# Dealing each expert's features six to a partition in a fused state-space and mixture-of-experts layer on Trainium2

## The chip, the cores and the metric

The kernel runs on one NeuronCore of one Trainium2 chip. The metric is the device time of one execution in microseconds (us). A core has five engines with instruction streams of their own: TensorE (PE in the profile, with its weight loads listed apart as PEld), VectorE (DVE), ScalarE (ACT), GpSimd (POOL) and SyncE (SP, which here only issues transfers). All numbers are float32.

## What is computed

There are 16 sequences of 256 tokens with 256 channels. For each the output is the input plus two branches, both fed by the layer-normed input `xn`:

```
xn = layernorm(x)
x  = x + ssm(xn) + moe(xn)

# ssm: proj, causal conv (4 taps), silu, then a scan over time with 512 features x 16 states
dts = softplus(dt @ W_dt + b_dt);  dA = exp(dts * A);  dBu = dts * Bm * hs
state = dA * state + dBu ;  y = sum_n state * C
out_ssm = ((y + hidden * D) * silu(gate)) @ W_out

# moe: 32 experts of 96 features, the 8 best of a softmax router per token
for e in range(32):
    w_e = sum(where(sel == e, rw, 0))
    acc += (silu(xn @ w_gate[e]) * (xn @ w_up[e])) @ w_down[e] * w_e
```

The change is in the second branch. The 32 x 96 = 3072 expert features of all experts are computed for every token; the routing weight `w_e` of a token (zero for an expert that it didn't choose) scales the features of expert e.

## The kernel before

One sequence is one round `b` of 16. Features lie on the 128 partitions, tokens along the free dimension. The 3072 expert features are 24 chunks of 128, and PE, ACT, POOL and DVE work on pairs of chunks `q` (12 pairs a round). Four groups `g` of 8 experts (768 features, 6 chunks, `CPG` = 6) share one tile of routing weights.

A pair goes through these steps. `gates` (line 496, two pairs at once) and `ups` (`expand`, line 483) multiply the transposed input `xnT` by the gate and up weights: four matmuls a pair and kind, with a 128x128 slice of the resident weights `wg_sb` or `wu_sb` as the loaded (stationary) operand and 256 tokens moving (line 490). `silu` (line 500) takes the gate product from PSUM to `sg` on ACT; `weigh` (line 506) multiplies `sg` by the routing weights `wr` on POOL; `combine` (line 511) multiplies by the up product into `h` on DVE; `down` (line 517) multiplies `h` by `wd_sb` and adds into `acc` over the whole round (line 525).

The routing weights of a round are computed with tokens on partitions, transposed on DVE, and written to a small array in device memory by four transfers (`send_weights`, line 456). `spread` (line 467) then reads them back so that each partition holds the row of the expert whose feature it carries. A chunk has 128 features and an expert 96, so chunks and experts don't meet: chunk 0 holds expert 0 and a third of expert 1, and so on. The pattern repeats after 4 experts and 3 chunks, so a group takes six transfers, of 32, 64 or 96 partitions, each of which fills two chunks. The tile is 128 x 6 x 256 numbers, with a ring of two tiles.

The state-space branch runs beside this: `project`, `conv_first`, `conv_rest`, `activate`, `params`, `widen` and `steps` prepare a round; `fetch` (line 634) spreads two states' rows of B and C over all partitions by a 512 KB transfer (`rep`, a ring of three tiles); `feed` (line 646) multiplies on POOL; `decay` (line 655) is the exponential on ACT; `scan` and `read` (lines 668 and 676) run on DVE; `collect` (line 686) adds to `y` by an accumulating transfer that POOL issues; `gate`, `fold`, `gated` and `project_out` finish it. `load_again`, `settle`, `finish` and `store` add the input and write the result.

The order of instructions on every engine comes from a planner that runs while the program is built. The class `Plan` (line 20) takes the steps with an engine, an assumed length, a due time, what they need, and which ring buffers they take and give back; it plays them forward and, whenever an engine is free, starts the ready step with the earliest due time (line 86). The due time is a base time (`ORIGIN`, `PERIOD`, `RATE`, `LEAD`) plus a constant for the kind of step, from the tables `DUE`, `FIRST` (first round), `SECOND` and `LAST`; `EARLY` says how long before its due time a step may become ready. The result is a fixed order for each engine; on the chip the instructions wait for each other by semaphores.

SP issues all loads and stores and the transfers of `spread`, `fetch`, `send_weights` and `send_params`, in the planned order. At the start it issues the first input (`load_x`), then router and projection weights, and later the expert weights in four groups of three kinds (`load_experts`, line 298).

Of the kernel before, what the change touches and what calls it, by code (L numbers as in the profile page):

```python
# [120 lines left out]
def mamba_moe_kernel(  # L121
# [30 lines left out]
    nc = tc.nc  # L152
    P = 128
    B, L, H = x.shape
# [4 lines left out]
    NE, _, I = w_gate.shape  # L159
# [6 lines left out]
    AHEAD = 3  # L166
# [3 lines left out]
    PARTS = 4  # L170
    EPG = NE // PARTS
    CPG = FC // PARTS
# [3 lines left out]
    SPP = SLOTS // PARTS  # L176
    FAR = 1e30
    SLOWEST = 1e-26
    ORIGIN = -7.2
    PERIOD = 79.1  # L180
    RATE = 79.0

    DUE = dict(
        load_x=-300.5, stats=-15.5, root=132.5, invert=-162.0, center=-75.0, norm=244.0,
        turn=-535.0, keep_turned=-94.0, route=-100.0, largest=-231.5, expo=221.0, choose=-1192.5,
        send_weights=-260.5, project=-51.5, conv_first=455.5, conv_rest=185.0, activate=-293.5,
        params=-209.0, keep_params=-266.0, send_params=-303.5, widen=-273.0, steps=-79.0,
        skip=120.0, inputs=-299.5, fetch=-252.5, feed=315.5, decay=-34.0, scan=539.0, read=55.9,
        collect=-257.0, spread=65.5, gates=-25.5, ups=669.0, silu=245.5, weigh=233.0,
        combine=-138.5, down=288.0, settle=-496.5, gate=50.5, gate_silu=216.0, fold=502.5,  # L190
        gated=894.5, project_out=-81.0, load_again=-68.0, finish=160.0,
    )
    EARLY = dict(
        load_x=175.0, load_experts=25.0, stats=37.0, turn=1.0, route=277.0, project=671.0,
    )

    FIRST = dict(
        route=179.5, largest=36.5, expo=-163.5, choose=655.5, project=409.0, conv_first=-563.0,
        conv_rest=-561.0, activate=218.5, params=-266.5, keep_params=285.0, widen=-51.5,
        steps=971.5, skip=-377.0, inputs=295.0, fetch=-161.5, feed=-360.0, decay=-135.0, scan=36.5,  # L200
        read=33.0, collect=-157.0, spread=-263.5, gates=-97.5, ups=-247.0, silu=-204.0,
        weigh=270.0, combine=402.0, down=53.0,
    )

    SECOND = dict(
        load_x=-132.5, stats=-1.0, root=-131.0, invert=-137.5, center=-86.0, norm=251.0,
        turn=267.0, keep_turned=-305.5, route=89.0, largest=-27.5, expo=-14.0, choose=46.0,
        send_weights=8.0, project=267.5, conv_first=36.5, conv_rest=-36.5, activate=-61.0,
        params=26.0, keep_params=178.5, send_params=13.0, widen=126.5, steps=-25.0, skip=225.5,
        inputs=-138.5, fetch=-56.0, feed=24.0, decay=7.0, scan=104.0, read=31.5, collect=-154.0,  # L210
        spread=8.0, gates=1.5, ups=-251.0, silu=46.5, weigh=-137.5, combine=48.0, down=100.5,
        settle=-112.0, gate=-10.0, gate_silu=-83.0, fold=99.0, gated=-152.0, project_out=-44.0,
        load_again=-35.0, finish=22.5,
    )

    LAST = dict(
        fetch=-123.0, feed=-25.0, decay=359.0, scan=571.0, read=-65.0, collect=-281.5,
        spread=-131.0, gates=216.5, ups=75.5, silu=445.0, weigh=-274.5, combine=448.0, down=296.5,
        settle=-10.0, gate=-75.5, gate_silu=105.5, fold=-115.5, gated=339.0, project_out=-460.5,
        finish=479.0,  # L220
    )
    LEAD = -28.0
    TOPK = 8
    EPS = 1e-5

# [5 lines left out]
    sb = ctx.enter_context(tc.tile_pool(name="sb", bufs=1))  # L231
# [2 lines left out]

    RINGS = dict(
        sk=1, xt=1, mv=1, st=1, std=1, xnT=3, nmax=1, rest=1, dt=1, hs=2, dts=2, y0=2, y1=2,
        rep=3, bu=3, pr=4, da=AHEAD, g=2, u=2, acc=1, wr=2, sg=3, h=2, gs=2, o=1,
    )
    taken = defaultdict(int)

    def take(pool, ring, shape, nm):
        i = taken[ring] % RINGS[ring]
        taken[ring] += 1
        return pool.tile(shape, F32, tag=f"{ring}_{i}", name=nm)
# [3 lines left out]
    live = {}  # L248
# [216 lines left out]


    def spread(b, g):
        wd = live["wd", b]
        wr = take(sb, "wr", [P, CPG, L], f"wr_{b}_{g}")
        half = EPG // 2  # L470
        for e in range(half):
            lo, hi = e * I, (e + 1) * I
            while lo < hi:
                c, r = divmod(lo, P)
                n = min(hi - lo, P - r)
                nc.sync.dma_start(
                    wr[r : r + n, c :: CPG // 2, :],
                    wd[g * EPG + e : (g + 1) * EPG : half, :].partition_broadcast(n),
                )
                lo += n  # L480
        live["wr", b, g] = wr

    def expand(b, q, kind):
        xs = live["xnT", b]
        w = {"g": wg_v, "u": wu_v}[kind]
        p = bank(f"p{kind}_{b}_{q}", kind).rearrange("p (j l) -> p j l", j=2)
        for j in range(2):
            c = 2 * q + j
            for hc in range(HC):
                nc.tensor.matmul(  # L490
                    p[:, j, :], w[:, hc, ts(c, P)], xs[:, hc, :],
                    start=(hc == 0), stop=(hc == HC - 1),
                )
        live[kind, b, q] = p
# [271 lines left out]
    b = 0  # L766
# [40 lines left out]
    for b in range(B):  # L807
# [54 lines left out]
        for g in range(GROUPS):  # L862
            at = t + PERIOD / GROUPS * g
            add("fetch", (b, g), "SP", 512 * KB, at, b, g, needs=[("send_params", b)],
                takes=[("rep", ("rep", b, g))], lands=5.5, early=14.0)

        for r in range(UNITS):
            k = UNITS * b + r
# [54 lines left out]
        add("load_again", (b,), "SP", 256 * KB, t, b, takes=[("o", ("o", b))], lands=8.0, early=25.0)  # L923
# [3 lines left out]
        add("gate", (b,), "PE", 8 * MM, t, b, gives=[xT],  # L927
            takes=[(r, (r, "gate", b, q)) for q in range(2) for r in ("g", "gs")],
            needs=[("keep_turned", b)] + ([] if b else [("load_in", 1)]), early=10.0)
# [10 lines left out]
        for q in range(PAIRED):  # L940
# [5 lines left out]
            gives=[("po", b)])  # L946
        add("store", (b,), "SP", 256 * KB, t + 100.0, b, needs=[("finish", b), ("settle", b)],
            gives=[("o", b)],
            lands=7.0)
    plan.issue()  # L950


# [30 lines left out]
```

## Time and profile before

| | |
|---|---|
| time, median of 3 runs | 1308.02 us (1305.14 to 1309.28) |
| span of the profiled execution, first to last instruction | 1309.5 us |
| instructions | 18902 |
| bytes moved by transfers | 268.80 MB, 205 GB/s on average |
| queue 0 (issued by POOL) | 124.80 MB, 50.4% of the time of 16 transfer engines |
| queue 1 (issued by SP and ACT) | 142.75 MB, 40.4% |
| mean granted TensorE clock | 0.993 |

The profile is of one execution of its own, whose span stands above; the times of the three runs are whole executions without its detail. In its rows, "xcount | busy, mean ns of one" tells how many instructions of a kind there were, how long their engine was busy with them altogether, and the mean length of one. Matmuls overlap in their records, so their pace is read from the starts of successive rows rather than from the mean length. One matmul of the program is two MATMUL records, each with a weight load (LDWEIGHTS) of its own.

### The profile page before, as it was taken

To read this page: it belongs to the slowest core of one execution; us is meant where nothing else is said; L and a number is where in the kernel's file an instruction comes from. 1 tells how busy PE (TensorE), PEld (TensorE's weight loads), DVE (VectorE), ACT (ScalarE), POOL (GpSimd) and SP (SyncE) were. 2 spreads that over 40 slices of the span, in tenths; PEclk is the share of its full clock that TensorE was granted. 3 is DMA by queue.
4 is the path that set the end of the run, shared out by engine and by line. 5 is a ranking of instruction groups with operands and counts; after the bars stand their busy time and mean duration, and the time that the engine had idled before them with its cause. 6 is when DMAs were issued, how large, how long until landed. Compare 5 with 4: busy or idle time off the path is not lost.

```text
span 1309.5 us, 18902 instructions
## 1 busy us (share of the span) xinstructions
PE 1288.9 (98%) x5978; PEld 1109.9 (85%) x5978; DVE 1157.5 (88%) x1719; ACT 1133.9 (87%) x1898; POOL 1181.6 (90%) x835
## 2 busy tenths in 40 slices
PE   9979999999999999999999999999999999999998
PEld 7868888887888888888888888888888888888887
DVE  3778989999899998989899898898989899899986
ACT  5878898997989989899898989989899898998883
POOL 1778999999999989999999898999999989998995
PEclk8999999999999999999999999999999999999999
DMA  9998899899999989999998988989899989998994
GB/s 248 241 230 191 189 237 195 215 206 211 201 222 198 226 199 200 199 212 206 199 215 188 213 191 206 225 189 209 185 216 216 197 193 203 217 210 193 202 221 94
DMA packets 169940, 268.80 MB, mean 205 GB/s; under 512 B 37840, under 2 KB 103920, under 8 KB 169840
## 3 DMA queue, kind: packets, MB, share of 16 engines
q0 software_dynamic: 36576, 124.80, 50.4%
q1 hardware_dynamic: 130624, 142.75, 40.4%
q8 instruction: 47, 0.77, 0.2%
q10 hardware_dynamic: 2640, 0.05, 0.1%
q14 instruction: 53, 0.43, 0.1%
HBM read 137.51 MB, written 5.24 MB: 109 GB/s over the span
## 4 chain that ended last, share of the span: by engine, by line
PE 63%; POOL 12%; DVE 8%; issue 6%; DMA 5%; ACT 4%; SPq 1%; POOLq 0%; DVEq 0%; ACTq 0%
PE acc L525 16%; PE pg L490 16%; PE pu L490 16%; POOL bu L649 6%; POOL sg L509 4%; PE px L574 3%; PE po L742 3%; PE ph L536 3%; DVE da L671 3%; PE pgate L716 3%; DMA y<-pr 2%; POOL y L688 2%; DVE hs L559 2%; DVE pr L683 2%; ACT da L663 2%
## 5 line engine op out<-in xcount | busy, mean ns | idle before, releaser
L649 POOL TENSOR_TENSOR bu<-rep,hs 128x1024 f32<-128x1024 f32 x256 | 716.4, 2924 | 59.7 <-DMA rep<-bcd 34.2
L671 DVE TENSOR_TENSOR_SCAN da<-da,bu 128x512 f32<-128x512 f32 x512 | 609.0, 1217 | 53.0 <-ACT da L663 44.8
L663 ACT ACTIVATE da<-dts,a_sb 128x256 f32<-128x256 f32 x1024 | 469.6, 473 | 84.6 <-DVE pr L683 61.9
L490 PE MATMUL pu<-xnT,wu_sb 128*128 128x256 f32 x1536 | 362.5, 382 | 5.8 <-DVE h L513 5.5
L525 PE MATMUL acc<-wd_sb,h 128*128 128x256 f32 x1536 | 364.2, 380 | 3.9 <-DVE h L513 3.8
L490 PE MATMUL pg<-xnT,wg_sb 128*128 128x256 f32 x1536 | 348.8, 380 | 3.1 <-DVE hs L559 1.5
L490 PEld LDWEIGHTS pu<-xnT,wu_sb 128*128 128x128 f32 x1536 | 292.6, 191 | 48.0 <-DVE h L513 7.5
L490 PEld LDWEIGHTS pg<-xnT,wg_sb 128*128 128x128 f32 x1536 | 291.0, 190 | 46.1 <-ACT sg L503 2.9
L525 PEld LDWEIGHTS acc<-wd_sb,h 128*128 128x128 f32 x1536 | 291.6, 190 | 45.1 <-DVE h L513 5.1
L509 POOL TENSOR_TENSOR sg<-sg,wr 128x512 f32<-128x512 f32 x192 | 326.3, 1922 | 2.3 <-ACT sg L503 2.3
L688 POOL DMA_DIRECT2D y<-pr x222 | 299.9, 1352 | 16.6 <-DVE da L671 5.8
L683 DVE TENSOR_TENSOR pr<-da,rep 128x512 f32<-128x512 f32 x448 | 294.0, 676 | 2.7 <-DVE pr L683 0.7
L663 ACT ACT_TABLE_LOAD x151 | 193.7, 1283 | 2.6
L513 DVE TENSOR_TENSOR h<-pu,sg 128x512 f32<-128x512 f32 x192 | 131.1, 683 | 58.9 <-POOL sg L509 31.8
L503 ACT ACTIVATE sg<-pg 128x512 f32<-128x512 f32 x192 | 105.3, 594 | 4.3 <-PE pg L490 2.1
L503 ACT ACT_TABLE_LOAD x81 | 103.9, 1283 | 2.9 <-PE pg L490 1.5
L732 POOL TENSOR_TENSOR y<-y,gs 128x512 f32<-128x512 f32 x30 | 79.4, 2816 | 0.2
L559 DVE SCALAR_TENSOR_TENSOR hs<-ph,small,hs 128x255 f32<-128x255 f32 (+2 forms) x192 | 76.0, 471 | 1.9 <-ACT hs L548 1.9
L707 POOL TENSOR_TENSOR y<-y 128x512 f32<-128x512 f32 x32 | 64.6, 2347 | 0.5 <-DMA y<-pr 0.5
L536 PE MATMUL ph<-xnT,win_sb 128*128 128x256 f32 x256 | 63.4, 392 | 0.0
L742 PE MATMUL po<-wout_sb,y 128*128 128x256 f32 x256 | 60.8, 380 | 1.0 <-DVE hs L559 1.0
L574 PE MATMUL px<-hs,wx_sb 128*32 128x256 f32 (+1 forms) x256 | 61.4, 387 | 0.0
(66 smaller groups left out, 863.4 us busy)
## 6 DMA issues: line engine op xcount, KB each, us to landing
y<-pr POOLq DMA_DIRECT2D x222, 512.0 KB, 7.0
rep<-bcd SPq DMA_DIRECT2D x128, 512.0 KB, 6.6
wr<-wd SPq DMA_DIRECT2D x128, 192.0 KB, 6.6
wr<-wd SPq DMA_DIRECT2D x128, 128.0 KB, 7.1
wr<-wd SPq DMA_DIRECT2D x128, 64.0 KB, 6.7
y<-sk POOLq DMA_DIRECT2D x32, 256.0 KB, 8.1
xt<-L_attn_input_states_dram SPq DMA_DIRECT2D x16, 256.0 KB, 4.9
o<-L_attn_input_states_dram SPq DMA_DIRECT2D x16, 256.0 KB, 6.9
```

Of the source, the lines that this page charges most:

```text
L490: nc.tensor.matmul(p[:, j, :], w[:, hc, ts(c, P)], xs[:, hc, :], start=(hc == 0), stop=(hc == HC - 1),)
L503: nc.scalar.activation(sg, live.pop(("g", b, q)), AF.Silu)
L509: nc.gpsimd.tensor_mul(sg, sg, wr[:, r : r + 2, :])
L513: nc.vector.tensor_mul(h, live.pop(("u", b, q)), live.pop(("sg", b, q)))
L525: nc.tensor.matmul(acc[:, s, :], h[:, j, ts(s, P)], wd_sb[:, c, :], start=(c == 0 and s == 0), stop=(c == FC - 1), skip_group_check=True,)
L536: nc.tensor.matmul(ph[:, j, :], win_sb[:, hc, ts(2 * q + j, P)], xs[:, hc, :], start=(hc == 0), stop=(hc == HC - 1),)
L559: nc.vector.scalar_tensor_tensor(cv[:, c, k:], ph[:, j, : L - k], cw[:, c, KC - 1 - k : KC - k], cv[:, c, k:], op0=ALU.mult, op1=ALU.add,)
L649: nc.gpsimd.tensor_mul(bu, live["rep", b, g][:, 0:1].to_broadcast([P, CPU, NG, L]), live["hs", b][:, ts(u, CPU), :].unsqueeze(2).to_broadc ...
L663: nc.scalar.activation(da[:, i, :], dts[:, c, :], AF.Exp, scale=a_sb[:, c, n : n + 1])
L671: nc.vector.tensor_tensor_scan(flat, flat, live["bu", k][:, j].rearrange("p n l -> p (n l)"), 0.0, op0=ALU.mult, op1=ALU.add,)
L683: nc.vector.tensor_mul(live["pr", k][:, :, j, :], live.pop(("da", m)), live["rep", b, g][:, 1])
L688: nc.gpsimd.dma_start(live["y", b, u].rearrange("p n c l -> p (n c l)"), live.pop(("pr", k)).rearrange("p n c l -> p (n c l)"), accum_op=A ...
```

## The change

There are three parts.

1. The 768 features of a group of 8 experts are dealt to the 128 partitions six at a time: partition p holds features 6p to 6p+5 of the group, and chunk r of the group is the r-th of the six. As 6 x 16 = 96, sixteen partitions hold exactly one expert, whatever the chunk. So `wr` shrinks to one row of 256 numbers per partition, one tile serves all six chunks, and `weigh` reads it for both chunks of a pair. `wd_sb` is loaded in the same dealing, six consecutive rows to a partition. The gate and up weights stay in memory as they were; the slice of a chunk now takes every sixth column.
2. `spread` is one transfer per group, from 8 rows, each repeated 16 times. The ring of `wr` has four tiles instead of two.
3. The tables of due times, the base times, the planner's assumed lengths of a few steps and the "early" limits are all new, so the order of instructions is another. The tables now name every kind of step.

```diff
@@ base times, rings
-    ORIGIN = -7.2
-    PERIOD = 79.1
-    RATE = 79.0
+    ORIGIN = -7.07
+    PERIOD = 79.07
+    RATE = 79.73
...
-    LEAD = -28.0
+    LEAD = -11.12
...
-        rep=3, bu=3, pr=4, da=AHEAD, g=2, u=2, acc=1, wr=2, sg=3, h=2, gs=2, o=1,
+        rep=3, bu=3, pr=4, da=AHEAD, g=2, u=2, acc=1, wr=4, sg=3, h=2, gs=2, o=1,
@@ weights
-    wd_v = w_down.rearrange("e i h -> (e i) h").rearrange("(c p) h -> p c h", p=P)
+    wd_v = w_down.rearrange("e i h -> (e i) h").rearrange("(g p c) h -> p g c h", p=P, c=CPG)
...
-            nc.sync.dma_start(wd_sb[:, ts(j, CPG), :], wd_v[:, ts(j, CPG), :])
+            nc.sync.dma_start(wd_sb[:, ts(j, CPG), :], wd_v[:, j])
...
-    wg_v = wg_sb.rearrange("p c e i -> p c (e i)")
-    wu_v = wu_sb.rearrange("p c e i -> p c (e i)")
+    wg_v = wg_sb.rearrange("p c (g e) i -> p c g (e i)", g=PARTS)
+    wu_v = wu_sb.rearrange("p c (g e) i -> p c g (e i)", g=PARTS)
@@ def spread(b, g):
-        wd = live["wd", b]
-        wr = take(sb, "wr", [P, CPG, L], f"wr_{b}_{g}")
-        half = EPG // 2
-        for e in range(half):
-            lo, hi = e * I, (e + 1) * I
-            while lo < hi:
-                c, r = divmod(lo, P)
-                n = min(hi - lo, P - r)
-                nc.sync.dma_start(
-                    wr[r : r + n, c :: CPG // 2, :],
-                    wd[g * EPG + e : (g + 1) * EPG : half, :].partition_broadcast(n),
-                )
-                lo += n
+        wr = take(sb, "wr", [P, L], f"wr_{b}_{g}")
+        rows = live["wd", b][ts(g, EPG), :]
+        nc.sync.dma_start(
+            wr,
+            rows.unsqueeze(1).to_broadcast([EPG, P // EPG, L]),
+        )
@@ def expand(b, q, kind):
-            c = 2 * q + j
+            g, r = divmod(2 * q + j, CPG)
             for hc in range(HC):
                 nc.tensor.matmul(
-                    p[:, j, :], w[:, hc, ts(c, P)], xs[:, hc, :],
+                    p[:, j, :], w[:, hc, g, r::CPG], xs[:, hc, :],
@@ def weigh(b, q):
-        g, r = divmod(2 * q, CPG)
-        sg, wr = live["sg", b, q], live["wr", b, g]
-        nc.gpsimd.tensor_mul(sg, sg, wr[:, r : r + 2, :])
+        sg, wr = live["sg", b, q], live["wr", b, 2 * q // CPG]
+        nc.gpsimd.tensor_mul(sg, sg, wr.unsqueeze(1).to_broadcast([P, 2, L]))
@@ assumed lengths (and the tables DUE, EARLY, FIRST, SECOND, LAST, all numbers new)
-        add("center", (b,), "POOL", 0.15, t, b, needs=[("invert", b)], gives=[("mv", b)])
+        add("center", (b,), "POOL", 0.74, t, b, needs=[("invert", b)], gives=[("mv", b)])
...
-        add("turn", (b,), "PE", 1.0, t, b, needs=[("norm", b)], gives=[x],
+        add("turn", (b,), "PE", 0.46, t, b, needs=[("norm", b)], gives=[x],
...
-        add("choose", (b,), "DVE", 1.35, t, b, needs=[("expo", b)], gives=[("pl", b)])
+        add("choose", (b,), "DVE", 1.8, t, b, needs=[("expo", b)], gives=[("pl", b)])
...
-            add("spread", (b, i), "SP", 3.0, e + RATE / PARTS * i, b, i,
-                needs=[("send_weights", b)], takes=[("wr", ("wr", b, i))], lands=6.0, early=20.0)
+            add("spread", (b, i), "SP", 0.55, e + RATE / PARTS * i, b, i,
+                needs=[("send_weights", b)], takes=[("wr", ("wr", b, i))], lands=6.0)
```

The limits `early=` written at `fetch`, `load_again` and `gate` move into the table `EARLY`, and `store` is assumed to land after 5 us instead of 7.

In the new order SP's first issues are: input of round 0, the input again for the sum (`o`), router, `wx_sb`, `wdt_sb`, first half of the projection weights `win_sb`, then gate and up weights of group 0. Before, they were: input, router, `win_sb`, `wx_sb`, `wdt_sb`, `o`, then gate and up weights. The four spreads of round 0 follow each other, and the down weights of group 3 and `wout_sb` come ahead of the fourth `fetch` of round 0, not after it. The same numbers of matmuls, DVE and POOL instructions are issued; ACT has 310 loads of function tables in place of 311.

More of the change, by code (lines that the diff above doesn't have):

```diff
@@ L178, in mamba_moe_kernel @@
     SLOWEST = 1e-26
-    ORIGIN = -7.2
-    PERIOD = 79.1
-    RATE = 79.0
+    ORIGIN = -7.07
+    PERIOD = 79.07
+    RATE = 79.73
     DUE = dict(
[L184 to L191, printed above, removed]
+        activate=-14372.8, center=-6022.0, choose=-4603.8, collect=439.7, combine=-4252.2,
+        conv_first=3168.6, conv_rest=-192.9, decay=-60.9, down=6788.6, expo=-1436.4,
+        feed=3333.9, fetch=-1632.2, finish=-4392.0, fold=4615.1, gate=58.4, gate_silu=6879.2,
+        gated=4038.3, gates=-31.6, grow=-5617.4, inputs=-3387.6, invert=-5277.5,
+        keep_params=-2167.6, keep_router=501.7, keep_turned=5837.8, keep_warm=-1115.3,
+        largest=9003.9, load_again=-5734.6, load_experts=-2.3, load_in=-982.1, load_out=795.2,
+        load_router=-4325.9, load_steps=-3249.6, load_x=-10931.1, norm=1112.7, params=-6418.4,
+        project=1679.9, project_out=-10551.0, read=-1220.9, root=473.6, route=-86.5,
+        scan=3318.4, send_params=-7387.5, send_weights=2123.1, settle=-8313.8, shrink=-1323.7,
+        silu=825.0, skip=6552.7, spread=-3397.9, stats=-15.7, steps=-100.9, store=-922.1,
+        turn=-7476.5, turn_router=-8372.6, ups=10848.0, warm=-2093.2, weigh=1953.2,
+        widen=-1497.8,
@@ L192, in mamba_moe_kernel @@
     )
     EARLY = dict(
-        load_x=175.0, load_experts=25.0, stats=37.0, turn=1.0, route=277.0, project=671.0,
+        fetch=640.7, gate=1299.0, load_again=92.1, load_experts=927.4, load_x=235.6,
+        project=1730.4, route=74.1, spread=676.2, stats=37.2, turn=696.4,
     )
     FIRST = dict(
-        route=179.5, largest=36.5, expo=-163.5, choose=655.5, project=409.0, conv_first=-563.0,
-        conv_rest=-561.0, activate=218.5, params=-266.5, keep_params=285.0, widen=-51.5,
-        steps=971.5, skip=-377.0, inputs=295.0, fetch=-161.5, feed=-360.0, decay=-135.0, scan=36.5,
@@ L201, in mamba_moe_kernel @@
-        read=33.0, collect=-157.0, spread=-263.5, gates=-97.5, ups=-247.0, silu=-204.0,
-        weigh=270.0, combine=402.0, down=53.0,
+        activate=-5051.7, center=3359.8, choose=3385.3, collect=-2418.9, combine=-651.0,
+        conv_first=-3188.7, conv_rest=-2390.5, decay=-5619.3, down=-1336.4, expo=-3322.8,
+        feed=-4122.0, fetch=-1012.2, finish=3889.5, fold=-1285.9, gate_silu=-5891.6,
+        gated=-2148.5, gates=-2070.4, grow=-3074.4, inputs=3084.1, invert=-584.2,
+        keep_params=2974.3, keep_router=1379.6, keep_turned=872.0, keep_warm=2059.0,
@@ new lines, in mamba_moe_kernel @@
+        largest=-383.9, load_again=-3137.3, load_experts=-544.8, load_in=527.9, load_out=-510.3,
+        load_router=-3260.2, load_steps=1596.7, load_x=-3180.0, norm=2309.9, params=2196.1,
+        project=-435.6, project_out=-819.6, read=-3426.6, root=1926.0, route=-4169.0,
+        scan=-765.8, send_params=-1899.2, send_weights=-4094.8, settle=-6592.4, shrink=-3667.0,
+        silu=2101.9, skip=-7064.2, spread=1725.8, stats=-4945.0, steps=5306.2, store=1161.2,
+        turn=1548.5, turn_router=-2691.0, ups=-1128.7, warm=2320.2, weigh=1292.4, widen=-5335.4,
@@ L203, in mamba_moe_kernel @@
     )
     SECOND = dict(
[L206 to L211, printed above, removed]
@@ L212, in mamba_moe_kernel @@
-        settle=-112.0, gate=-10.0, gate_silu=-83.0, fold=99.0, gated=-152.0, project_out=-44.0,
-        load_again=-35.0, finish=22.5,
+        activate=1363.6, center=5288.3, choose=-2707.0, collect=2929.7, combine=93.7,
+        conv_first=-1837.1, conv_rest=245.9, decay=-2805.7, down=1615.8, expo=-3565.0,
+        feed=47.7, fetch=-259.0, finish=1698.3, fold=3961.1, gate=-2.5, gate_silu=1581.6,
+        gated=-2111.7, gates=3.8, grow=3106.2, inputs=-7001.4, invert=2267.3,
+        keep_params=-2175.5, keep_router=5004.5, keep_turned=-4251.2, keep_warm=-2646.9,
@@ new lines, in mamba_moe_kernel @@
+        largest=762.0, load_again=-1191.8, load_experts=2931.9, load_in=-2153.9,
+        load_out=4446.9, load_router=-1201.8, load_steps=6183.9, load_x=1973.4, norm=-245.5,
+        params=-5534.1, project=-1488.6, project_out=-2558.6, read=-1221.3, root=-985.0,
+        route=-3620.8, scan=-2069.4, send_params=-105.8, send_weights=-1404.1, settle=-2671.6,
+        shrink=957.6, silu=936.8, skip=2537.1, spread=-40.0, stats=-1890.4, steps=6579.7,
+        store=-4883.0, turn=1686.5, turn_router=-4505.2, ups=-993.4, warm=-387.1, weigh=-3945.0,
@@ L214, in mamba_moe_kernel @@
+        widen=1228.0,
     )
     LAST = dict(
[L217 to L220, printed above, removed]
+        activate=1503.4, center=494.7, choose=2763.9, collect=-2798.7, combine=-370.8,
+        conv_first=-360.7, conv_rest=2449.7, decay=3267.6, down=103.8, expo=796.6, feed=-1091.1,
@@ new lines, in mamba_moe_kernel @@
+        fetch=-806.9, finish=548.8, fold=-6205.6, gate=1254.4, gate_silu=-3602.0, gated=-2289.2,
+        gates=722.7, grow=-7026.0, inputs=-2371.9, invert=-6552.9, keep_params=8627.2,
+        keep_router=-11148.1, keep_turned=-2071.8, keep_warm=4928.2, largest=1310.8,
+        load_again=2399.1, load_experts=-1641.7, load_in=1613.2, load_out=-2363.5,
+        load_router=-4152.8, load_steps=-547.8, load_x=2289.5, norm=2363.5, params=-2855.8,
+        project=-325.0, project_out=-7292.8, read=2291.1, root=-4060.4, route=7.1, scan=-1753.5,
@@ L221, in mamba_moe_kernel @@
+        send_params=-2121.9, send_weights=1084.8, settle=-4449.8, shrink=1688.8, silu=2395.8,
+        skip=2760.0, spread=-21.7, stats=-24.0, steps=3040.6, store=-3553.9, turn=2814.5,
+        turn_router=397.3, ups=5131.5, warm=-4246.5, weigh=-655.2, widen=615.9,
     )
-    LEAD = -28.0
+    LEAD = -11.12
     TOPK = 8
@@ L864, in mamba_moe_kernel @@
             add("fetch", (b, g), "SP", 512 * KB, at, b, g, needs=[("send_params", b)],
-                takes=[("rep", ("rep", b, g))], lands=5.5, early=14.0)
+                takes=[("rep", ("rep", b, g))], lands=5.5)
         for r in range(UNITS):
@@ L922, in mamba_moe_kernel @@
                 table="silu")
-        add("load_again", (b,), "SP", 256 * KB, t, b, takes=[("o", ("o", b))], lands=8.0, early=25.0)
+        add("load_again", (b,), "SP", 256 * KB, t, b, takes=[("o", ("o", b))], lands=8.0)
         add("settle", (b,), "DVE", 0.62, e, b, needs=[("down", b, PAIRS - 1), ("load_again", b)],
@@ L928, in mamba_moe_kernel @@
             takes=[(r, (r, "gate", b, q)) for q in range(2) for r in ("g", "gs")],
-            needs=[("keep_turned", b)] + ([] if b else [("load_in", 1)]), early=10.0)
+            needs=[("keep_turned", b)] + ([] if b else [("load_in", 1)]))
         add("gate_silu", (b,), "ACT", 1.09, t, b, needs=[("gate", b)],
@@ L948, in mamba_moe_kernel @@
             gives=[("o", b)],
-            lands=7.0)
+            lands=5.0)
     plan.issue()
```

## The prediction

> **What bounds the kernel now.** First the totals of the page, to see whether one engine is full.
>
> ```profile
> PE 1288.9 (98%) x5978; PEld 1109.9 (85%) x5978; DVE 1157.5 (88%) x1719; ACT 1133.9 (87%) x1898; POOL 1181.6 (90%) x835
> ```
>
> PE is busy nearly all the time, but its ends are modelled, so I check it by its cadence. The timeline of PE (start, length, engine, line, operation) gives the same step of two successive rounds:
>
> ```profile
> 871.56 3.84 PE L574 MATMUL px<-hs,wx_sb 128*32 128x256 f32 x16
> 950.91 3.84 PE L574 MATMUL px<-hs,wx_sb 128*32 128x256 f32 x16
> ```
>
> A round takes 79.35 us, and the start of that step repeats to 0.01 us from 554.17 to 1030.26: PE alone sets the pace there. Sixteen rounds at 79.35 are 1269.6 us. The first projection matmul starts at 10.68 and the last matmul ends at 1305.7, 1295.0 us in which PE does all of this but the first turn and routing (about 1.3 us by their rows): 1295.0 - 1268.3 = 26.7 us are lost. That is the ceiling for any gain that doesn't shorten a round. Next, where it is lost: the waits of PE, and what they go back to on SP and POOL.
>
> ```profile
> 61.92 2.45 SPq L637 DMA_DIRECT2D rep<-bcd  x1
> ...
> 74.00 4.65 POOL L649 TENSOR_TENSOR bu<-rep,hs 128x1024 f32<-128x1024 f32 x2 [7.54 <-DMA rep<-bcd]
> ```
>
> ```profile
> 55.44 3.72 PE L490 MATMUL pg<-xnT,wg_sb 128*128 128x256 f32 x16 [0.62 <-ACT sg L503]
> 81.30 2.51 PE L525 MATMUL acc<-wd_sb,h 128*128 128x256 f32 x8 [2.83 <-DVE h L513]
> 89.31 1.99 PE L490 MATMUL pu<-xnT,wu_sb 128*128 128x256 f32 x8 [0.88 <-DVE h L513]
> 96.97 3.78 PE L490 MATMUL pu<-xnT,wu_sb 128*128 128x256 f32 x8 [3.08 <-DVE h L513]
> 100.55 1.91 PE L597 MATMUL pdt<-dt,wdt_sb 128*128 128x256 f32 x4
> 102.25 2.32 PE L525 MATMUL acc<-wd_sb,h 128*128 128x256 f32 x8
> 104.41 3.62 PE L490 MATMUL pg<-xnT,wg_sb 128*128 128x256 f32 x16
> ```
>
> In brackets is the idle time before a row and what ended it. The fourth fetch of round 0 was issued at 61.92, behind the expert weights, and POOL waited 7.54 us for it; DVE's scans stood behind that, ACT's exponentials behind the scans, the next `silu` behind those, and PE then waited for `h`. The four waits are 7.4 us. After two of them PE is also slow: eight matmul records take 1.73 us from start to start in the full stretch, but 2.30 from 81.30 and 3.58 from 96.97, and the rows at 100.55 and 102.25 lose 0.84 and 0.43 us. That is 3.7 us more (the granted clock from 60 to 110 us is 0.90). So 11.1 us go in this one place. The named waits of PE after 110 us add up to some 6 us, none above 1.1.
>
> **The strided weight load.** Now `wg_sb` and `wu_sb` are read with a step of six numbers, in 2 x 1536 loads, 192 a round. No load of the profile has a step, so I look for how fast plain ones go.
>
> ```profile
> 33.90 0.97 PE L413 MATMUL pl<-rwT,xnT 128*128 128x32 f32 x8
> 34.71 1.11 PE L597 MATMUL pdt<-dt,wdt_sb 128*128 128x256 f32 x4
> ...
> 44.29 3.62 PE L490 MATMUL pg<-xnT,wg_sb 128*128 128x256 f32 x16
> ```
>
> ```profile
> L490 PEld LDWEIGHTS pu<-xnT,wu_sb 128*128 128x128 f32 x1536 | 292.6, 191 | 48.0 <-DVE h L513 7.5
> L490 PEld LDWEIGHTS pg<-xnT,wg_sb 128*128 128x128 f32 x1536 | 291.0, 190 | 46.1 <-ACT sg L503 2.9
> ```
>
> The routing matmuls move only 32 columns, so their loads set the pace: eight in 34.71 - 33.90 = 0.81 us, 101 ns each, for the same 128x128 tile. In the expert matmuls (1.73 us for 8 records) the spacing is 216 ns. A load may thus become 216/101 = 2.13 times as long before PE, which has nothing else to hide it, slows at all; past that every nanosecond costs 3072 ns, 3.1 us per ns, and the cover is gone for good. A gain is excluded, since the moving side sets the pace. The low end is 0; the high end is the recorded length doubled without overlap, 2 x 190 - 216 = 164 ns, x 3072 = +505 us. I take 0, from the nearest row: same tile and type, at a pace that leaves room for double.
>
> One rule speaks against the change here. The Trainium skill, "SBUF — State Buffer", Door 1, says that the memory works in lines of 16 bytes, that at least two hits on a line are needed for full rate, and that a stride of up to 4 float32 is free. A step of 24 bytes hits each line once, so by the rule there is a penalty, of a size that it doesn't state. If it halves the rate, an estimate from that page and the 101 ns gives 202 ns and still no cost; if it is larger, the rule wins. No row before shows it.
>
> **Traffic of the routing weights.**
>
> ```profile
> q1 hardware_dynamic: 130624, 142.75, 40.4%
> ...
> rep<-bcd SPq DMA_DIRECT2D x128, 512.0 KB, 6.6
> wr<-wd SPq DMA_DIRECT2D x128, 192.0 KB, 6.6
> wr<-wd SPq DMA_DIRECT2D x128, 128.0 KB, 7.1
> wr<-wd SPq DMA_DIRECT2D x128, 64.0 KB, 6.7
> ```
>
> 384 transfers with 128 x (192 + 128 + 64) KB = 50.3 MB become 64 of 128 KB, 8.4 MB. By bytes that is 41.9/142.75 of 40.4%, some 12 points of a share that stands at 0.91 to 0.95. SP loses 320 issues at a median of 0.6 us. In the full stretch this buys nothing: PE waits for no transfer there. In the first 110 us it bears on the fourth fetch. Counting bytes ahead of it in SP's order: before, 14.7 MB, of which 2.3 are routing weights; after, 14.1 MB, since 0.5 MB of routing weights remain but the last down weights (0.75) and `wout_sb` (0.5) are now ahead. At the 229 GB/s of that stretch it comes 2.3 us earlier, and behind it 0.75 MB each of spread and down weights and the 0.5 MB no longer stand before the fifth, so POOL catches up faster. Of the 11.1 us I take half, -5.5. Ends: -11.1, all of it; and +5.5, if the six broadcast transfers cost little because their source is one row, so that the 1.25 MB moved ahead come on top (1.25 MB at 229 GB/s); what is then late is the same feed, and with it `h`.
>
> After 110 us I take half of the named 6 us, -3: waits that go back to late transfers shrink with the load, those that come from ACT's order do not. Ends: -6, and +4, two waits of the largest kind (about 2 us with the slow restart), since the order is new.
>
> **The start.** `win_sb` moves from the third place on SP to the sixth, past `o`, `wx_sb` and `wdt_sb`. SP's sixth issue stood at 6.41 us, held by the completion of earlier transfers, and the third at 1.73. The landing of the first `win_sb` load must be the 4.5 us of the two listed (4.5 and 9.4), since 9.4 would have come after its use at 10.68. So 6.41 + 4.5 = 10.9, +0.2 us; with the median 7.0, 13.4, +2.7. The input of round 0 also shares its time with `o`. I take +0.7, ends 0 and +2.7. The up weights now are first in line, but at SP's same places.
>
> **At nothing.** `weigh` on POOL keeps its 192 instructions of 512 columns at 1922 ns; the only doubly broadcast row, `bu`, takes 2924 ns for 1024, so a gain of at most 0.46 us each (88 us of POOL) and no loss by any row; POOL is 90% busy, PE covers it. `spread` as one transfer should land like the 64 to 192 KB ones, 6.6 to 7.1 us, and the four-deep ring frees SP from waiting on POOL's `weigh`, which held its spreads for 138 us. The same skill's page "DMA: Bandwidth & Descriptors", on why a DMA adds 16 to its semaphore, says that the number of engines must divide the slowest dimension of both sides; with 8 source rows that is 8 of 16. No row shows it. The four loads of down weights stand at the start, with PE waiting for none. The order of PE from round 8 to 13 is the old one by distances (16.3 us of matmuls from turn to projection, 1.7 from `params` to `widen`); rounds 1 to 6 and the last differ. The last twelve steps of PE are again twelve of 1.73 us, with the gate projection among them. One table load less is 1.3 us of ACT, not on the path.
>
> **Sum.** On the profiled span: 1309.5 + 0 - 5.5 - 3.0 + 0.7 = 1301.7. The span lies 1.5 us above the median of the runs, so 1300.
>
> **Rivals.**
> A (0.57), the forecast: loads stay hidden and the beginning gets thinner. Alone its range is 1290 to 1306, from taking nearly all or little of 11.1 + 6.
> B (0.22), slower: the strided load comes to more than 216 ns. For it speaks the step itself, on PE at 98%; against it the 101 ns. At 2.5 times, 253 ns: 37 x 3072 = 113 us, 1421; at 220 ns already 1308 - 8 + 12 = 1312. It decides from 2.13 times on.
> C (0.21): the lost time wasn't traffic's. The waits that PE names are for `h`, behind ACT's order; the new order moves them rather than removes them, gains 0 to 5 in one place and gives it back in rounds 1 to 6, where a mean of 1 us a round would be enough. 1308, within 1303 to 1314. For it: the fourth fetch is nearly as late by bytes. Against: the queues have 12 points less to do.
>
> A measurement of this kernel tells 0.3% from no change, some 4 us. Faster: 0.53 of A and 0.02 of C, 0.55. Same: 0.04 of A and 0.11 of C, 0.15. Slower: 0.22 of B and 0.08 of C, 0.30. The range, 1288 to 1330, leaves out most of B, some 0.17, and a little below.
>
> **What would show it.** Right: the spacing of `pg` and `pu` stays at 1.73 us for eight, the cadence at 79.35, queue 1 falls below 30%, and POOL's wait for `rep` near 66 to 74 us shrinks. If the spacing grows beyond 1.73, B holds and the rest hardly matters. If it stays and PE still waits 10 us or more before 110 us, C holds. A late start shows as a first `ph` well after 10.7.

## The result and the profile after

| | before | after |
|---|---|---|
| time, median | 1308.32 us (1305.14 to 1309.28, 4 runs) | 1315.95 us (1315.23 to 1316.9, 4 runs) |
| span of the profiled execution | 1309.5 us | 1313.4 us |
| mean granted clock | 0.993 | 0.998 |

The ratio after/before is 1.006, with a 95% interval of 1.0044 to 1.0076: the changed kernel is slower by 0.6%. The forecast was 1300 us, faster.

First the totals, the queue of SP's transfers and the chain that ended last, from the page of the changed kernel:

```profile
PE 1301.6 (99%) x5978; PEld 1210.1 (92%) x5978; DVE 1160.4 (88%) x1719; ACT 1132.8 (86%) x1897; POOL 1183.4 (90%) x835
...
q1 hardware_dynamic: 81472, 100.78, 28.4%
...
PE 94%; ACT 3%; DVE 1%; DMA 1%; issue 0%; POOL 0%; ACTq 0%; DVEq 0%; POOLq 0%
```

The transfers are lighter by the 42 MB that were counted, 28.4% for 40.4%. The other engines have the same work as before. PE has gained 12.7 us of busy time with the same 5978 matmul records, and its weight loads 100 us. PE is now 94% of the last chain (63% before): hardly anything but PE's own pace is left to explain the end. The costliest groups of the same page tell which weight loads grew (busy time and mean ns of one stand after the first bar):

```profile
L505 PEld LDWEIGHTS pu<-xnT,wu_sb 128*128 128x128 f32 x1536 | 355.0, 308 | 4.8 <-PE pg L505 0.7
...
L505 PEld LDWEIGHTS pg<-xnT,wg_sb 128*128 128x128 f32 x1536 | 350.7, 309 | 2.0 <-ACT gs L741 1.0
...
L539 PEld LDWEIGHTS acc<-wd_sb,h 128*128 128x128 f32 x1536 | 292.5, 191 | 36.5
```

Only the loads with the step of six did, from 190 or 191 to 308 or 309 ns; `wd_sb`, read without a step, stayed at 191. And the timeline of PE from 700 to 800 us shows what that does to the pace (start, length, operation, records):

```profile
700.07 3.74 PE L505 MATMUL pg<-xnT,wg_sb 128*128 128x256 f32 x16
703.64 1.89 PE L756 MATMUL po<-wout_sb,y 128*128 128x256 f32 x8
...
708.92 3.84 PE L588 MATMUL px<-hs,wx_sb 128*32 128x256 f32 x16
...
742.64 1.94 PE L505 MATMUL pu<-xnT,wu_sb 128*128 128x256 f32 x8
744.41 1.89 PE L539 MATMUL acc<-wd_sb,h 128*128 128x256 f32 x8
746.14 1.96 PE L505 MATMUL pu<-xnT,wu_sb 128*128 128x256 f32 x8
...
789.75 3.84 PE L588 MATMUL px<-hs,wx_sb 128*32 128x256 f32 x16
```

Sixteen strided records take 703.64 - 700.07 = 3.57 us from start to start, 223 ns each, where plain ones take 216. The eight of `pu` take 1.77, the eight of `acc` behind them still 1.73. With 192 strided records a round that is some 1.3 us, and the round, from `px` to `px`, is 80.83 us for 79.35: +1.48. Over sixteen rounds that would be 23.7 us.

The hoped-for part is there too. From PE's list of waits over the whole run (engine, waiting line, releaser: total, times, longest):

```profile
PE px L588 <- ACT sg L518: 2.1, 1, 2.1
...
PE pu L505 <- DVE h L527: 0.5, 1, 0.5
```

The 9.3 us for `h` in this list before have become one wait of 0.5. From 60 to 110 us, before and after:

```profile
60.00:110.00 50.00, 43.21 (x175) 35.11 (x174) 38.30 (x50) 36.60 (x63) 37.41 (x24) 0.90 0.95 229
```

```profile
60.00:110.00 50.00, 49.52 (x225) 47.27 (x224) 44.12 (x58) 46.08 (x79) 46.53 (x35) 1.00 0.83 172
```

The columns are the window, its length, busy time and instructions of PE, PEld, DVE, ACT and POOL, clock, share of the transfer engines, GB/s. PE was idle for 6.8 us here and now for 0.5, and its clock is no longer lowered (1.00 for 0.90). So the stall is gone, and the pace has cost more than that.

### The profile page after: what moved, and what is told of

Read it like the earlier page. It is cut to its first block, busy times and chain, and to the rows that moved or that the text cites. A ratio compares the mean times of both kernels' runs of the same rounds, so it can differ in the third digit from the quotient of the medians.

```text
span 1313.4 us, 18427 instructions
## 1 busy us (share of the span) xinstructions
PE 1301.6 (99%) x5978; PEld 1210.1 (92%) x5978; DVE 1160.4 (88%) x1719; ACT 1132.8 (86%) x1897; POOL 1183.4 (90%) x835
## 3 DMA queue, kind: packets, MB, share of 16 engines
q1 hardware_dynamic: 81472, 100.78, 28.4%
## 4 chain that ended last, share of the span: by engine, by line
PE 94%; ACT 3%; DVE 1%; DMA 1%; issue 0%; POOL 0%; ACTq 0%; DVEq 0%; POOLq 0%
PE pg L505 25%; PE pu L505 25%; PE acc L539 24%; PE px L588 5%; PE ph L550 4%; PE po L756 4%; PE pgate L730 4%; PE pdt L611 2%; ACT da L677 1%; PE pl L435 1%; DVE da L685 1%; ACT L677 0%; PE pt L420 0%; DMA win_sb<-in_L_attn_W_in_dram 0%; ACT L518 0%
## 5 line engine op out<-in xcount | busy, mean ns | idle before, releaser
L505 PE MATMUL pu<-xnT,wu_sb 128*128 128x256 f32 x1536 | 370.3, 387 | 0.5 <-DVE h L527 0.5
L505 PEld LDWEIGHTS pu<-xnT,wu_sb 128*128 128x128 f32 x1536 | 355.0, 308 | 4.8 <-PE pg L505 0.7
L505 PE MATMUL pg<-xnT,wg_sb 128*128 128x256 f32 x1536 | 358.6, 387 | 0.7 <-ACT gs L741 0.7
L505 PEld LDWEIGHTS pg<-xnT,wg_sb 128*128 128x128 f32 x1536 | 350.7, 309 | 2.0 <-ACT gs L741 1.0
L523 POOL TENSOR_TENSOR sg<-sg,wr 128x512 f32<-128x512 f32 x192 | 308.4, 1882 | 1.3 <-ACT sg L518 1.3
L746 POOL TENSOR_TENSOR y<-y,gs 128x512 f32<-128x512 f32 x30 | 65.9, 2657 | 0.2
```

The source lines that it names most:

```text
L505: nc.tensor.matmul(p[:, j, :], w[:, hc, g, r::CPG], xs[:, hc, :], start=(hc == 0), stop=(hc == HC - 1),)
L523: nc.gpsimd.tensor_mul(sg, sg, wr.unsqueeze(1).to_broadcast([P, 2, L]))
```

## The experiments

### Taking the three parts apart

**e1_step1** keeps everything of the changed kernel but the step of the slice.

```diff
-                    p[:, j, :], w[:, hc, g, r::CPG], xs[:, hc, :],
+                    p[:, j, :], w[:, hc, g, ts(r, P)], xs[:, hc, :],
```

> The changed kernel with one edit: the weight slice of a chunk is 128 neighbouring columns again, everything else (order, traffic, dealing of the down weights and of the routing weights) as changed. So the gate and up products are those of other features than the ones the routing and down weights belong to. Theory S (the step of six in the weight loads costs the 1.48 us by which a round is longer, 80.83 against 79.35): the weight load's record falls from 308 to about 190 ns, eight matmul records of pg or pu take 1.73 us again, a round takes 79.35 us, and the time is 1316 - 16 x 1.48 = about 1292 us. Rival X (the rounds are longer for another reason, the routing weights read twice on POOL or the new order): the round stays at 80.8 us and the time at 1314 to 1318 us.

Measured: 1296.12 us (1294.62 to 1297.12), ratio to before 0.9905 (0.9891 to 0.9919). Its groups of weight loads and its timeline of PE:

```profile
L505 PEld LDWEIGHTS pg<-xnT,wg_sb 128*128 128x128 f32 x1536 | 291.6, 190 | 41.6 <-ACT gs L741 1.6 <-ACT sg L518 0.3
```

```profile
859.31 3.84 PE L588 MATMUL px<-hs,wx_sb 128*32 128x256 f32 x16
938.66 3.84 PE L588 MATMUL px<-hs,wx_sb 128*32 128x256 f32 x16
```

Loads at 190 ns, the round at 79.35 us: the step alone is what the changed kernel lost, and it costs 1315.95 - 1296.12 = 19.8 us. That is less than sixteen times 1.48. From first `ph` to last matmul, the changed kernel takes 1298.2 - 1292.0 = 6.2 us more than sixteen rounds at its pace, and this one 1279.9 - 1268.3 = 11.6: a slower PE is kept waiting less. That wins back some 5 us by these two profiles, and 23.7 - 19.8 = 3.9 us by the times. The expected 1292 us was too low by as much.

**e2_light** is the opposite part alone: the old order, plain weights, the new single spread and `weigh`.

```diff
...
-        wr = take(sb, "wr", [P, CPG, L], f"wr_{b}_{g}")
-        half = EPG // 2
...
-                nc.sync.dma_start(
-                    wr[r : r + n, c :: CPG // 2, :],
...
+        wr = take(sb, "wr", [P, L], f"wr_{b}_{g}")
+        rows = live["wd", b][ts(g, EPG), :]
+        nc.sync.dma_start(
+            wr,
+            rows.unsqueeze(1).to_broadcast([EPG, P // EPG, L]),
+        )
...
-        nc.gpsimd.tensor_mul(sg, sg, wr[:, r : r + 2, :])
...
+        nc.gpsimd.tensor_mul(sg, sg, wr.unsqueeze(1).to_broadcast([P, 2, L]))
```

> The kernel before in its old order, with the routing weights as one transfer of 128 KB a group and one row a partition; weight slices and down weights stay as before, so the products are weighted by rows of other experts. Theory T (the early stall is made by the bytes of the routing weights): the four early waits of PE (7.4 us, 11.1 with the slow restart) mostly go, POOL's wait of 7.5 us for the fourth fetch shrinks below 3, and the time is 1294 to 1300 us. Rival O (the new order removed the stall, the bytes did not): POOL still waits 5 us or more for the fourth fetch and the time is 1304 to 1310 us.

Measured: 1290.89 us (1290.48 to 1294.11), ratio 0.9874 (0.9856 to 0.9892). The light spread alone is worth 17 us, twice the 8.5 of the prediction, and the time lies below the 1294 to 1300 expected. And the old order with it is 5.2 us faster than the new order with it (e1, which also has the ring of four and the dealt down weights); the two intervals just touch. What the spread changed shows on SP first. SP's timeline of before, and then that of e2 (start, time at the head of the queue, number of transfers):

```profile
19.99 8.10 SPq L476 DMA_DIRECT2D wr<-wd  x12
...
36.30 7.16 SPq L476 DMA_DIRECT2D wr<-wd  x6
```

```profile
20.57 1.75 SPq L470 DMA_DIRECT2D wr<-wd  x2
...
32.56 1.16 SPq L470 DMA_DIRECT2D wr<-wd  x1
...
53.42 0.37 SPq L629 DMA_DIRECT2D rep<-bcd  x1
```

Eighteen spreads held SP for 15.3 us ahead of the fourth fetch; three hold it for 2.9. The fetch leaves 8.5 us earlier, at 53.42 for 61.92 (and not 12.4, since SP now waits 2.2 us ahead of it for DVE to give back a tile of `rep`). POOL has no wait for `rep` from 55 to 110 us, and PE's clock from 60 to 110 us is 1.00. What that is worth shows between two `px`, as PE's order is the same. In e2:

```profile
59.49 3.84 PE L566 MATMUL px<-hs,wx_sb 128*32 128x256 f32 x16
...
141.58 3.84 PE L566 MATMUL px<-hs,wx_sb 128*32 128x256 f32 x16
```

That is 82.09 us, where before took 93.04 (62.54 to 155.58): 10.95 us less.

**e3_stride_only** is the third: before, with the slices of step six and nothing else.

```diff
...
-            c = 2 * q + j
+            g, r = divmod(2 * q + j, CPG)
...
-                    p[:, j, :], w[:, hc, ts(c, P)], xs[:, hc, :],
+                    p[:, j, :], w[:, hc, g, r::CPG], xs[:, hc, :],
```

> The kernel before in its old order and with its old transfers, with the step of six in the gate and up weight slices alone; the down and routing weights are not dealt to match, so the products are of other features than those weights belong to. Theory S: a round takes 80.83 us and the time is 1308 + 24 = 1332 us, less what the old stalls give back because PE is later, so 1322 to 1332. Rival X: about 1308 us.

Measured: 1321.65 us (1320.31 to 1322.8), ratio 1.0101 (1.0086 to 1.0115). The loads are at 308 ns, the round at 80.83 us, and POOL waits for `rep` as before, 33.7 us in all. Here too the 23.7 us of the rounds show only in part in the time, 14, since the slack beyond the rounds shrinks: from first `ph` to last matmul e3 takes 1306.1 - 1292.0 = 14.1 us more than sixteen rounds at its pace, where before took 26.7.

### Which step is free

The record of a load got 118 ns longer, and the spacing of the matmuls 7. So the step was varied. **e7_step2** and **e8_step4** change the slice of the changed kernel:

```diff
-                    p[:, j, :], w[:, hc, g, r::CPG], xs[:, hc, :],
+                    p[:, j, :], w[:, hc, g, r : r + 2 * P : 2], xs[:, hc, :],
```

```diff
-                    p[:, j, :], w[:, hc, g, r::CPG], xs[:, hc, :],
+                    p[:, j, :], w[:, hc, g, r : r + 4 * P : 4], xs[:, hc, :],
```

> The changed kernel with a step of two numbers (8 bytes) in the gate and up weight slices; the products are those of other features. The record of a weight load was 190 ns at a step of one, 251 at three and 308 at six. Theory L (by 16-byte lines touched: 32, 64, 96, then 128) gives 221 ns; a theory by distance, 20 to 30 ns a step, gives 214 to 220. Round 79.35, span near 1295.

> The changed kernel with a step of four numbers (16 bytes); the products are those of other features. Theory L: each column has a line of its own as at six, 308 ns, round 80.8 us, span near 1313. Theory by distance: 265 to 280 ns, below the matmuls' pace, round 79.4 and span near 1296.

**e4_three** deals three features to a partition, groups of 4 experts, so a step of three and a tile of two rows per partition, filled by four transfers of 64 KB.

```diff
...
-        wr = take(sb, "wr", [P, L], f"wr_{b}_{g}")
-        rows = live["wd", b][ts(g, EPG), :]
...
+        wr = take(sb, "wr", [P, 2, L], f"wr_{b}_{g}")
+        rows = live["wd", b][ts(g, EPG), :].rearrange("(f e) l -> e f l", f=2)
+        for e in range(EPG // 2):
+            nc.sync.dma_start(
+                wr[ts(e, 2 * P // EPG)], rows[e].partition_broadcast(2 * P // EPG)
+            )
...
-                    p[:, j, :], w[:, hc, g, r::CPG], xs[:, hc, :],
+                    p[:, j, :], w[:, hc, g, r :: CPG // 2], xs[:, hc, :],
...
```

> The changed kernel with features dealt three to a partition in groups of four experts (the step is 12 bytes in place of 24), a row of routing weights serves three chunks, a tile of two rows a partition filled by four transfers of 64 KB for 8 experts; the planner's tables as changed. Theory L (the load's time goes with the number of 16-byte lines it touches: 128 at a step of six, 96 at three, 32 at one): the load takes 0.75 of its present pace, about 167 ns, below the 216 ns of the matmuls, and the time is 1291 to 1295 us with a round of 79.35. Theory P (any step pays the same): a round of 80.8 us and 1314 to 1318 us. Of the 17 MB of routing weights, twice as many as in the changed kernel, both expect under 2 us.

Their weight loads, in the listing of groups of steps two, three and four:

```profile
L505 PEld LDWEIGHTS pg<-xnT,wg_sb 128*128 128x128 f32 x1536 | 301.5, 196 | 31.9 <-ACT gs L741 1.6 <-ACT sg L518 0.3
```

```profile
L506 PEld LDWEIGHTS pg<-xnT,wg_sb 128*128 128x128 f32 x1536 | 334.8, 251 | 3.0 <-ACT gs L745 1.5 <-ACT sg L519 0.5
```

```profile
L505 PEld LDWEIGHTS pg<-xnT,wg_sb 128*128 128x128 f32 x1536 | 366.9, 329 | 1.1
```

| step | bytes | record of a load | round | time |
|---|---|---|---|---|
| 1 (e1) | 4 | 190 ns | 79.35 us | 1296.12 |
| 2 (e7, one run) | 8 | 196 | 79.35 | 1295.63 |
| 3 (e4) | 12 | 251 | 79.41 | 1298.06 |
| 4 (e8, one run) | 16 | 328 | 82.78 | 1342.79 |
| 6 (after) | 24 | 308 | 80.83 | 1315.95 |

Neither theory fits. At two, 196 ns lie below what either had (214 to 221), and step four is worse than six, where one had them equal and the other had four at 265 to 280 ns. In the timeline of PE of step four the sixteen records take 717.48 - 713.75 = 3.73 us, 233 ns each:

```profile
713.75 3.90 PE L505 MATMUL pg<-xnT,wg_sb 128*128 128x256 f32 x16
717.48 1.89 PE L756 MATMUL po<-wout_sb,y 128*128 128x256 f32 x8
```

So the cost isn't a matter of distance. Up to step three the 216 ns of a matmul hide the longer load; at four and six they don't. What makes sixteen bytes worse than 24 was not tried. e4 itself, 1298.06 us (1295.3 to 1299.65) or 0.9919 (0.9904 to 0.9934) of before, lies above the 1291 to 1295 expected, but its rounds are nearly as short as expected: the dealing can be had almost without its price.

### What was late: bytes or transfers

The fourth fetch could be late for the bytes ahead of it or for the time SP spends to issue. **e9_bytes** takes before and fills the same tile by one transfer of 768 KB a group.

```diff
...
-                nc.sync.dma_start(
-                    wr[r : r + n, c :: CPG // 2, :],
-                    wd[g * EPG + e : (g + 1) * EPG : half, :].partition_broadcast(n),
-                )
...
+        nc.sync.dma_start(wr, wd[g : g + 26 : 5, :].partition_broadcast(P))
```

> The kernel before, with the tile of routing weights filled by one transfer of 768 KB a group (six rows of 1 KB to each of 128 partitions) in place of six that move the same bytes; the rows are some six experts' rows and not those of the features, so the weighting is another. Theory B (the stall before 110 us is made by the bytes): POOL still waits some 5 us or more for the fourth fetch and the time stays at 1303 to 1308 us. Rival Q (it is made by SP's issues, 6 a group, each held in the queue): the time is near the light run, 1291 to 1296.

**e10_issues** takes e2 and fills its tile of 128 KB by eight transfers of 16 KB (the edit is shown against e2).

```diff
-        nc.sync.dma_start(
-            wr,
-            rows.unsqueeze(1).to_broadcast([EPG, P // EPG, L]),
-        )
+        n = P // EPG
+        for e in range(EPG):
+            nc.sync.dma_start(
+                wr[ts(e, n)], live["wd", b][g * EPG + e].partition_broadcast(n)
+            )
```

> The kernel before with the light tile (one row a partition, 128 KB a group), filled by eight transfers of 16 KB, 512 in all where the kernel before has 384; weight slices and down weights as before, so the products are weighted by rows of other experts. Theory B: as the light run with one transfer, 1290 to 1294. Rival Q: 1302 us or more.

Measured: e9 1303.4 us (1301.8 to 1306.36), ratio 0.9976 (0.9963 to 0.9988); e10 1301.83 us (1299.74 to 1303.66), ratio 0.9954 (0.9941 to 0.9966). Few transfers with the old bytes win 3 or 4 us, the new bytes in many transfers 6, both together 17. Neither theory holds by itself: e9's time is at the low end of what the bytes alone were to give, but POOL's wait for the fourth fetch is gone, as by the rival; e10's time is close to the rival's 1302. The fourth fetch on SP in e9, and the spreads and the fourth fetch in e10:

```profile
56.00 1.35 SPq L627 DMA_DIRECT2D rep<-bcd  x1
```

```profile
20.94 8.78 SPq L471 DMA_DIRECT2D wr<-wd  x16
...
36.93 9.53 SPq L471 DMA_DIRECT2D wr<-wd  x8
...
60.93 2.46 SPq L629 DMA_DIRECT2D rep<-bcd  x1
```

When the fetch leaves is mainly a matter of transfers: 61.92 and 60.93 us with six and eight a group, 56.00 and 53.42 with one. For the same bytes, fewer transfers bring it 5.9 us (e9 against before) and 7.5 us (e2 against e10) earlier; for the same number of transfers, fewer bytes 2.6 us (e2 against e9). POOL still waits 3.78 us for it in e10 (7.54 before) and not at all in e9. The full stretch doesn't split so cleanly: from 110 to 600 us PE is busy for 487.05 us in e9 and 489.61 in e10 (e2 489.86), from 600 to 1200 for 598.76 and 596.63 (e2 598.86). Either of the two loads, left in, keeps 2 to 3 us of small waits there, and why in these places stays open.

### The new order, and a better kernel

**e6_start** is e1 with SP's first loads in the old sequence (the edit is shown against e1).

```diff
-        for st in self.order():
+        steps = self.order()
+        first = [("load_x", 0), ("load_router",), ("load_in", 0), ("load_steps",), ("load_again", 0)]
+        steps.sort(key=lambda st: first.index(st["name"]) if st["name"] in first else len(first))
+        for st in steps:
```

> The changed kernel with neighbouring columns (the run called step 1, 1296.1 us, whose gate and up products are those of other features) and, on SP alone, the first five loads in the order of the kernel before: input, router, win_sb, wx_sb, wdt_sb, o. All other orders stay. Theory N (what the new order costs against the old one, 1296.1 against 1290.9, is lost at the start, where the first projection waited for win_sb until 11.56 us against 9.43, and ran slowly after the wait): first projection near 9.5 us, the round's params step near 20.5 instead of 23.8, time 1292 to 1294. Rival W (it is lost in the waits of the new order later, 2.3 us before params of round 1 and 1.2 before a gate at 1146 us): 1295 to 1297.

Measured: 1294.9 us (1293.76 to 1295.33), ratio 0.9903 (0.9887 to 0.9919). The first projection matmuls in e1, and in this kernel, from the timelines of PE:

```profile
11.56 5.38 PE L550 MATMUL ph<-xnT,win_sb 128*128 128x256 f32 x16 [1.32 <-DMA win_sb<-in_L_attn_W_in_dram]
```

```profile
9.28 3.70 PE L553 MATMUL ph<-xnT,win_sb 128*128 128x256 f32 x16
```

The late load is gone, 2.3 us at the start and 1.7 of slow running after it, but the next matmuls then wait 1.7 us for `wu_sb`. The time moves by 1.2 us, with ranges that overlap, and the ratio to the runs of before beside it by 0.0002: no gain clear of noise, near the rival's 1295 to 1297. So the start doesn't account for the 5.2 us between e1 and e2. The trace of e1 also names a wait of 2.3 us at 57.19 (`px` for `sg`), after which that step is slow (5.42 us for 3.84), and one of 1.2 us (`pg` for `gs`). They are about the right size, but no run took them away, so where the 5.2 us go is not shown. The new order with the old, heavy tiles was not tried.

**e5_old_order_three** joins what was good: the old order and the dealing of three, with four transfers of 64 KB.

```diff
...
-        wr = take(sb, "wr", [P, CPG, L], f"wr_{b}_{g}")
...
+        wr = take(sb, "wr", [P, 2, L], f"wr_{b}_{g}")
...
-                    p[:, j, :], w[:, hc, ts(c, P)], xs[:, hc, :],
+                    p[:, j, :], w[:, hc, g, r :: CPG // 2], xs[:, hc, :],
...
```

> The kernel before in its old order, with features dealt three to a partition (a step of 12 bytes), a tile of two rows of routing weights a partition, filled by four transfers of 64 KB for 8 experts. If the two gains and losses add (old order with light traffic 1290.9 us; a step of three adds 0.06 us a round, as 79.41 against 79.35 in the run of three with the new order), the time is 1291 to 1294 us. If the new order was needed for the dealt form, 1298 us or more.

Measured: 1295.13 us (1293.37 to 1299.34), ratio 0.9909 (0.9889 to 0.9929), just above the 1291 to 1294 expected. It is faster than both kernels: by 12 us than before (1307.11 in the same group of runs), 21 than after. Against e4 the intervals overlap, and e2, with its plain weights, is faster still. It still has four transfers a group, and POOL waits 11.2 us for `rep`.

**e11_old_order_three_2** halves the number, with two transfers of 128 KB, each of four rows repeated 32 times (the edit is shown against e5).

```diff
-        rows = live["wd", b][ts(g, EPG), :].rearrange("(f e) l -> e f l", f=2)
-        for e in range(EPG // 2):
+        for f in range(2):
+            rows = live["wd", b][ts(2 * g + f, EPG // 2), :]
             nc.sync.dma_start(
-                wr[ts(e, 2 * P // EPG)], rows[e].partition_broadcast(2 * P // EPG)
+                wr[:, f, :], rows.unsqueeze(1).to_broadcast([EPG // 2, 2 * P // EPG, L])
```

> The kernel before in its old order with features dealt three to a partition, and its two rows of routing weights a partition filled by two transfers of 128 KB, each from four rows repeated 32 times, in place of four of 64 KB. The run with four took 1295.1 us and POOL waited 11.2 us for fetches in it, against 1.7 in the light run at 1290.9. If SP's issues are what the four cost, 1291 to 1294 us; if the bytes (twice the light run's), 1295.

Measured: 1300.3 us (1299.65 to 1305.48), ratio 0.9952 (0.9935 to 0.9968). A miss: half the transfers, but 5 us slower than e5, with POOL's wait for `rep` at 12.8 us, though the fourth fetch leaves at 53.44 us for 54.92. A transfer here fills all 128 partitions with one row each, from four rows, where one of e5 fills 32 partitions with two rows each, so more than the number differs. The profile lists no time to landing for these spreads, and why they are worse stays open.

## Why the prediction was wrong

**The strided weight load: the step that failed.** The term was 0, on the ground that plain loads pace at 101 ns where 216 were to be had, so that a load could grow to 2.13 times. The frame agrees with the runs as far as they go: the step of six paces at 223 ns, and if the load alone sets that pace, it is 2.2 times the 101, just beyond 2.13. (A strided load without 256 columns to hide it was not run.) The size was wrong. The choice of 0 rested on the nearest row, and that row has no step; it could tell the room, but nothing of how a step fills it. The bounds, 0 to +505 us, were wide enough to say so. By 3.1 us per ns the 7 ns come to 22 us; the rounds give 23.7, and e1 gives 19.8 in the time. Rival B is what happened, not at its 2.5 times but near its smallest case, 220 ns and 1312 us.

Of the rule quoted against the change, from the Trainium skill's "SBUF — State Buffer", Door 1, one half agrees with the rows and one doesn't. Two hits to a line of 16 bytes, as step two has, are nearly free (196 for 190 ns), and the larger steps pay. But a stride of four float32 is not free here: three costs 61 ns of the load's record and four 138, the most of all. The estimate made from the page, half the rate and still hidden, did not come true; its alternative, a larger penalty, did.

**Traffic before 110 us: right in sign, too small, and by the wrong count.** The fetch was to come 2.3 us earlier by bytes ahead of it. In e2 it left 8.5 us earlier, most of it by SP's time for issues, which the prediction had in hand (320 issues at a median of 0.6 us) and left out of what stands ahead of the fetch. There the 18 spreads took 15.3 us. In the changed kernel the fetch leaves 3.4 us earlier (58.54 for 61.92), held at the end by a wait of 4.5 us for a tile of `rep` and no longer by spreads, and the stall is gone there too. Not half of 11.1 came but nearly all: the 10.95 us between the two `px` of e2. (The 11.1 were a little short: 16 records from 83.60 us took 4.83 where others take 3.62.)

**Traffic after 110 us: right in sign, too small.** Forecast -3, within 4 and -6. From 110 to 1200 us PE's idle time falls from 6.1 us before to 1.3 in e2, 4.8 us. From the `px` of the third round to that of the last, with slow running included, before needs 1040.46 us (155.58 to 1196.04) and e2 1033.92 (141.58 to 1175.50), 6.5 less and just beyond the range.

**The start: near the number, partly by luck.** +0.7 was set for `win_sb` in the sixth place, and the first `ph` came at 11.44 for 10.68. But SP issued that load at 5.34 us and not at 6.41, and it took longer than the 4.5 us assumed: `ph` waited for it. And 10.68 is the latest start seen with the old sequence of loads. The runs with it begin `ph` from 9.28 (e5, e6) to 10.68 us, with the old tiles at 9.29 (e3); those with the new one from 10.95 to 12.02. So the move delays `ph` by about 1.7 us on average, and by e6 costs next to nothing in the time. The length of the first `ph` varies too (5.51 us before, 3.70 in e2, but also in e3), so 1.8 of the 19.6 us that e2's profile gains between first `ph` and last matmul are not the tiles'.

**The new order: left out.** Rounds 8 to 13 were compared and found alike, and the rest was priced only in the start and in rival C. By e1 and e2 it costs 5.2 us with light traffic. Rival C's claim that the lost time wasn't traffic's fell: e2 has the old order and lost the stall.

**At nothing.** `weigh` stayed at nothing on the path: 1882 for 1922 ns each. The four-deep ring did not free SP: it still waits 110.2 us for `weigh` in its spreads, 138.1 before. The cadence and queue 1 were named as what would show it, and did: "if the spacing grows beyond 1.73, B holds" is how the trace reads. But the rest did matter: the step alone took 1321.65 us (e3), and with the other parts it takes 1315.95.

The sum with what was measured runs before 1308, light spread -17, new order +5, step of six +20: 1316. It closes by construction, as each term is the difference of two runs on the way from before over e2 and e1 to after.

## What to carry over

Where an engine is at 98%, a layout that makes its operand strided has to be priced at that operand first, and a plain row gives the room for it, not the price; one run with the step alone (e3) shows the sign. A step that changes which data lie on which partition often comes in several sizes: three to a partition kept four fifths of the bytes saved (33.6 of 42.0 MB) at 0.06 us a round, six lost more than all of it. Ahead of a transfer that something waits for, count the issuing queue's time as well as the bytes.

## What was not expected of the hardware

- The record of a 128x128 float32 weight load grows with the step to 196, 251, 328 and 308 ns at 2, 3, 4 and 6: sixteen bytes are worse than 24, in the record and in the pace (233 against 223 ns). Two and four were run once each.
- The record overstates the price. It is 190 ns for a load whose pace alone is 101, and 251 ns still fit behind matmuls spaced 216. Where the matmuls slow down, the record is longer than their spacing by about as much as for the plain load alone: 308 - 223 = 85 and 328 - 233 = 95, against 190 - 101 = 89 ns. By that, an estimate, a load of step three takes some 160 ns.
- In the loaded beginning SP's time for a spread hardly depends on its size: 15.3 us for 18 of 64 to 192 KB (before), 18.3 for 24 of 16 KB (e10), 3.4 for three of 768 KB (e9).
